# A gated cross-attention and quantized feed-forward block: VectorE's and ScalarE's order in the attention written out, side work cut small, weights rounded on ScalarE

## The chip, the cores and the metric

The kernel runs on one core of one Trainium2 chip. The metric is the device time of one execution in microseconds; lower is better. The engines named below are TensorE (PE, the matmuls; PEld is its weight load), VectorE (DVE), ScalarE (ACT), GpSimd (POOL) and SyncE (SP, which here issues nearly all DMAs). Each engine executes its own list of instructions in order and waits on semaphores for the others.

## The reference

x has 4096 rows (2 x 2048) of 512 numbers, the context 2 x 77 rows of 512. Two gated residual steps follow each other:

```python
x = x + tanh(g_xattn) * attention(layernorm(x), ctx, ctx)      # 16 heads of 32, 77 keys, all fp32
x = x + tanh(g_ffn)   * ffn(layernorm(x))
# ffn: qlinear(512 -> 2048), exact gelu, qlinear(2048 -> 512), where
#   scale = max(max|x|, 1e-6) / 127 ;  xq = round(x / scale)   # one scale for a whole tensor
#   qlinear = (xq @ wq.T + b) * (s_w * s_x)
```

Four one-number scales are needed: of the normalized input of the feed-forward, of its hidden values, and of the weights w1 and w2. Each needs the maximum over its whole tensor before anything of it can be rounded.

## The kernel before, in words

The rows are cut into NB = 8 blocks of 512, each of NT = 4 tiles of 128 rows. The kernel has three stages: the attention of all blocks (within `with actx`), the first feed-forward matmul of all blocks (`ph`, line 664), and the second (`pf`, line 728).

The attention is a pipeline. A loop over blocks i and steps s = 0 to 7 (lines 508 to 577) handles in each step one half (two row tiles) of one group of four heads. In the source, one step does this:

- even s: `apply_v` (378): `pc`, the weights times v for the group before, and ScalarE's copy to `cT`;
- `softmax` (329) for the step two ahead: scores `ps` on PE; on VectorE the maximum `mx` (347) and the difference `e` (351); the exponential on ScalarE (357); on VectorE the sum `sm` (359) and its inverse `rs` (361); the product on GpSimd (362);
- `transpose_a` (368): PE transposes this step's `e` into `pta`, ScalarE copies it to `aT` (376), twice;
- even s: `project_o` (394) of the block before: `po`, and on VectorE the addition to x (404);
- odd s: `project_q` (316) for coming steps: `pq`, and ScalarE's `qT` with its bias (327).

PSUM tiles `pq`, `po`, `pc`, `pk`, `pvv`, `pm` and `pg` share two buffers with the tag `pp`; `pta` and `ptx` share two; `ps` has two.

Beside this pipeline lies side work. `norm(i+2)` (267) takes the mean and variance of a block that comes up (in step 6; that of block 1 in block 0's step 1), and `spread_rstd` sends the inverse deviation through DRAM to a row that `scale_x` (GpSimd) multiplies into the transposed x. `center_wq` (288) takes the column mean off wq once, in block 1. `norm2_stats` and `norm2_max` (408, 413) take mean, variance and the largest normalized value of a finished block, all four tiles at once, in step 7. `weight_step` (454) loads the raw weights piece by piece (1 MB, 128 x 2048 on chip), takes the maximum of each piece (440), gets the scale (`diagonal_of` 174, `scale_of` 182 with the matmul `pg_w`), and rounds by adding and subtracting a magic number: `quantize` (210) does both passes on VectorE (212 in place, 213 to bf16). The raw weights and the blocks of x share eight buffers of one pool; pieces of w2 are loaded, dropped and loaded again.

What sets the order: within `manual_schedule`, the engines named follow the source exactly. In the lead-in (block 0's statistics, transposes and keys) these are VectorE, PE and ScalarE; from line 503 on it is PE alone. There VectorE's, ScalarE's, GpSimd's and SP's instructions are put in order by the framework's scheduler, and `tc.issue_after(ins)` only keeps a piece of side work behind a given instruction of the same engine. The scheduled order is fixed when the program is built.

After the loop, the last block's `po`, statistics and maxima come tile by tile, then the scale `s_x`, the rounding and transposing of block 0 (`xq0`, `px`, `xqT0`), and the feed-forward begins.

Of the kernel before, what the change touches and what calls it, by code (L numbers as in the profile page):

```python
# [15 lines left out]
P = 128  # L16
# [26 lines left out]
def tile_flamingo_gated_block(  # L43
# [115 lines left out]
    xmax = const.tile([P, NB - 1 + NT], F32, name="xmax")  # L159
    hmax = const.tile([P, NB * GT * 2 + 1], F32, name="hmax")  # L160

    def layernorm_stats(xb, mv, rstd, name):

        n = xb.shape[1]
        st = small.tile([P, n, 6], F32, tag="st", name=f"st_{name}")
        for t in range(n):
            nc.vector.bn_stats(st[:, t, :], xb[:, t, :])  # L167
            nc.vector.bn_aggr(mv[:, t, :], st[:, t, :])
        ve = small.tile([P, n], F32, tag="ve", name=f"ve_{name}")
        last = nc.vector.tensor_scalar(ve, mv[:, :, 1], EPS, None, ALU.add).ins  # L170
        nc.gpsimd.tensor_tensor(rstd, ve, mhalf[:, :n], ALU.pow)  # L171
        return last

    def diagonal_of(maxima, name):

        m = const.tile([P, 1], F32, name=f"m_{name}")
        nc.vector.tensor_reduce(m, maxima, AX.X, ALU.max)  # L177
        diag = small.tile([P, P], F32, tag="diag", name=f"diag_{name}", bufs=1)
        nc.vector.tensor_scalar(diag, ident, m, None, ALU.mult)
        return diag  # L180
# [38 lines left out]
    with actx:  # L219
# [44 lines left out]
        rstd_row = {}  # L264
        ln, xnT, qT, aT, cT, es = {}, {}, {}, {}, {}, {}

        def norm(i):

            mv = small.tile([P, NT, 2], F32, tag="mv", name=f"mv{i}")
            rstd = small.tile([P, NT], F32, tag="rstd", name=f"rstd{i}")  # L270
            layernorm_stats(X[i], mv, rstd, f"a{i}")
            ln[i] = mv, rstd
# [15 lines left out]
        def center_wq():  # L288

            total = work.tile([P, D], F32, tag="xn", name="wq_total")  # L290
            nc.gpsimd.tensor_tensor(total, wq_sb[:, 0, :], wq_sb[:, 1, :], ALU.add)
            for kc in range(2, KC):
                nc.gpsimd.tensor_tensor(total, total, wq_sb[:, kc, :], ALU.add)
            pm = ps_p.tile([P, D], F32, tag="pp", name="pm")
            nc.tensor.matmul(pm, ones, total, start=True, stop=True)
            for kc in range(KC):
                w = wq_sb[:, kc, :]
                nc.vector.scalar_tensor_tensor(w, pm, -1.0 / D, w, ALU.mult, ALU.add)

        def transpose_x(i, t):  # L300
            mv, rstd = ln[i]
            if t == 0:
                xnT[i] = work.tile([P, KC, TB], F32, tag="xnT", name=f"xnT{i}", bufs=2)
            xn = work.tile([P, D], F32, tag="xn", name=f"xn{i}_{t}")
            nc.vector.tensor_scalar(
                xn, X[i][:, t, :], mv[:, t, 0:1], rstd[:, t : t + 1], ALU.subtract, ALU.mult
            )
            pt = ps_t.tile([P, KC, P], F32, tag="pt", name=f"ptx{i}_{t}")
            for kc in range(KC):
                nc.tensor.transpose(pt[:, kc, :], xn[:, kc * P : (kc + 1) * P], ident)  # L310
# [18 lines left out]
        def softmax(i, s):  # L329
# [19 lines left out]
            e4 = e.rearrange("p u (j k) -> p u j k", j=HG)  # L349
            last = {}  # L350
            last["DVE"] = nc.vector.tensor_tensor(  # L351
# [4 lines left out]
            ).ins  # L356
            last["ACT"] = nc.scalar.activation(e, e, AF.Exp, scale=SCALE).ins  # L357
# [4 lines left out]
            last["POOL"] = nc.gpsimd.tensor_tensor(  # L362
                e4, e4, rs[:, :, :, None].to_broadcast([P, 2, HG, NK]), ALU.mult
            ).ins
            es[i, s] = e4
            return last
# [27 lines left out]
        def project_o(i, t):  # L394
            po = ps_p.tile([P, D], F32, tag="pp", name=f"po{i}_{t}")
            for g in range(NG):
                nc.tensor.matmul(  # L397
                    po,
# [5 lines left out]
            nc.vector.scalar_tensor_tensor(  # L404
                X[i][:, t, :], po, tg[:, 0:1], X[i][:, t, :], ALU.mult, ALU.add
            )

        def norm2_stats(i, t0=0, t1=NT):
            return layernorm_stats(
                X[i][:, t0:t1, :], mean2[:, i, t0:t1, :], rstd2[:, i, t0:t1], f"f{i}_{t0}"  # L410
            )

        def norm2_max(i, t0=0, t1=NT):

            tm = small.tile([P, NT], F32, tag="tm", name=f"tm{i}_{t0}")
            for t in range(t0, t1):
                xn = work.tile([P, D], F32, tag="xn", name=f"xf{i}_{t}")
                normalize2(xn, i, t)
                nc.vector.tensor_reduce(  # L419
                    tm[:, t - t0 : t - t0 + 1], xn, AX.X, ALU.max, apply_absolute_value=True  # L420
                )
            k = i if t1 - t0 == NT else NB - 1 + t0
            return nc.vector.tensor_reduce(
                xmax[:, k : k + 1], tm[:, : t1 - t0], AX.X, ALU.max
            ).ins
# [4 lines left out]
        wraw, wmax, wdiag = {}, {}, {}  # L430

        def load_w(name, src, pieces):
            for j in pieces:
                wraw[name, j] = big(f"raw_{name}{j}")
                nc.sync.dma_start(wraw[name, j], kchunks(src(j)))

        def weight_max(name, j):
            if j == 0:
                wmax[name] = const.tile([P, 4], F32, name=f"max_{name}")
            nc.vector.tensor_reduce(  # L440
                wmax[name][:, j : j + 1],
                wraw[name, j],
                AX.XY,
                ALU.max,
                apply_absolute_value=True,
            )

        def w1_piece(j):
            return w1T[:, j * TB : (j + 1) * TB]

        def w2_piece(j):
            return w2T[j * TB : (j + 1) * TB, :]

        def weight_step(i, s):
            j, odd = divmod(s, 2)
            if i == 1 and odd:
                weight_max("w1", j)
            if i in (2, 4) and s == 0:
                name = "w1" if i == 2 else "w2"
                s_w[name], inv_w[name] = scale_of(wdiag[name], name, ps_p, "pp")  # L460
            if i == 2 and odd:
                quantize(w1q[:, :, j * TB : (j + 1) * TB], wraw["w1", j], inv_w["w1"])
            if i == 3 and odd:
                weight_max("w2", j)
                if j < 2:
                    load_w("w2", w2_piece, [j + 2])
                else:
                    load_w("w2", w2_piece, [j - 2])
            if i in (1, 3) and s == 2 * NG - 1:
                name = "w1" if i == 1 else "w2"  # L470
                wdiag[name] = diagonal_of(wmax[name], name)
            if i == 4 and odd:
                quantize(w2q[:, j * KC : (j + 1) * KC, :], wraw["w2", j], inv_w["w2"])
                if j in (1, 2):
                    load_w("w2", w2_piece, [j + 1])

        ordered = {mybir.EngineType.DVE, mybir.EngineType.PE, mybir.EngineType.Activation}
        with tc.manual_schedule(engines=ordered):
            ln[0] = (
                small.tile([P, NT, 2], F32, tag="mv", name="mv0"),  # L480
                small.tile([P, NT], F32, tag="rstd", name="rstd0"),
            )
            pk = {}
            for t in range(NT + 1):
                if t < NT:
                    layernorm_stats(
                        X[0][:, t : t + 1, :],
                        ln[0][0][:, t : t + 1, :],
                        ln[0][1][:, t : t + 1],
                        f"a0_{t}",  # L490
                    )
                if t > 0:
                    transpose_x(0, t - 1)
                if t in (2, 3):
                    pk[t - 2] = project_k(0, t - 2)
            place_k(0, 0, pk[0])
            pk[2] = project_k(0, 2)
            place_k(0, 1, pk[1])
            project_q(0, 0)
            place_k(0, 2, pk[2])  # L500
            pk[3] = project_k(0, 3)
            place_k(0, 3, pk[3])
        actx.enter_context(tc.manual_schedule(engines={mybir.EngineType.PE}))
        softmax(0, 0)
        softmax(0, 1)
        project_q(0, 1)
        project_v(0)
        for i in range(NB):
            for s in range(2 * NG):
                g, odd = divmod(s, 2)  # L510
                if not odd and s > 0:
                    apply_v(i, g - 1)
                elif not odd and i > 0:
                    apply_v(i - 1, NG - 1)
                if s + 2 < 2 * NG:
                    last = softmax(i, s + 2)
                elif i + 1 < NB:
                    last = softmax(i + 1, s + 2 - 2 * NG)
                for u in range(2):
                    transpose_a(i, s, u)  # L520
                if i == 0 and s == 2:


                    with tc.issue_after(last["ACT"]):
                        nc.scalar.activation(tg, tg, AF.Tanh)
                    with tc.issue_after(last["POOL"]):
# [285 lines left out]
```

## Time and profile before

| | |
|---|---|
| median of 3 runs | 661.34 us (660.38 to 662.39) |
| the profiled execution | 661.28 us |
| its span, first to last instruction | 659.5 us |
| mean granted PE clock | 0.981 |
| attention, to the last `pc` | 0 to 399.7 us |
| first `ph` matmul | 424.9 us |
| first `pf` matmul | 542.6 us |

In the profile, "busy" is the time in which an engine has an instruction under way. A line such as `aT<-pta` reads "writes aT from pta", x8 counts merged instructions, and a bracket at the end of a line gives the idle time of that engine just before, and the instruction on another engine that ended it. Times on a timeline are from the span's start.

### The profile page before, as it was taken

What the parts mean: (1) busy time and instruction counts of PE and PEld (TensorE: products, weight loads), DVE (VectorE), ACT (ScalarE), POOL (GpSimd) and SP (SyncE); (2) the same over time, 40 slices, a digit from 0 to 9 for tenths busy, and PEclk for the clock granted to TensorE, in tenths of its full rate; (3) what the DMA queues carried; (4) which work ended last, traced back from release to release, by engine and by line L of the source; (5) the groups of instructions that cost most, each with busy time, mean ns of one, the idle gap of its engine ahead of it and who ended that gap; (6) DMA issues with size and microseconds to landing.
All of it is one profiled execution on the core that took longest, in us unless ns stands there. A gap on an engine that the chain in (4) does not pass through costs nothing.

```text
span 659.5 us, 8041 instructions
## 1 busy us (share of the span) xinstructions
PE 620.7 (94%) x2954; PEld 311.1 (47%) x2954; DVE 508.3 (77%) x805; ACT 325.8 (49%) x439; POOL 235.7 (36%) x188
## 2 busy tenths in 40 slices
PE   5999999799999799999999999599999979999997
PEld 5556455455445455455455544244444434444443
DVE  5687678968979968957866767899999779877541
ACT  2355444243344243344434341289998879655430
POOL 2147345255264255264363332000000008997000
PEclk9999999899999899999999999699999999999999
DMA  9922220133252233320000000079999208799952
GB/s 282 375 89 72 74 65 0 17 123 132 80 181 76 80 128 129 80 65 1 16 1 1 0 17 0 8 264 326 295 328 348 58 0 341 255 355 347 336 199 80
DMA packets 51454, 92.76 MB, mean 141 GB/s; under 512 B 22155, under 2 KB 26251, under 8 KB 45784
## 3 DMA queue, kind: packets, MB, share of 16 engines
q1 hardware_dynamic: 50312, 91.58, 40.8%
q10 hardware_dynamic: 1104, 0.69, 0.4%
q8 instruction: 23, 0.38, 0.2%
q14 instruction: 15, 0.12, 0.1%
HBM read 57.11 MB, written 31.47 MB: 134 GB/s over the span
## 4 chain that ended last, share of the span: by engine, by line
PE 73%; DVE 22%; POOL 2%; ACT 1%; issue 1%; DMA 1%; DVEq 0%; POOLq 0%; ACTq 0%
PE pf L728 17%; PE ph L664 17%; PE po L397 11%; PE pq L319 11%; PE pta L375 6%; PE ps L338 5%; PE pc L384 3%; DVE e L351 3%; DVE mx L347 3%; DVE st_a L167 2%; DVE tm L419 2%; DVE xf L197 2%; DVE sm L359 2%; DVE st_f L167 2%; PE pk L231 1%; POOL rstd L171 1%
## 5 line engine op out<-in xcount | busy, mean ns | idle before, releaser
L362 POOL TENSOR_TENSOR e<-e,rs 128x616 f32<-128x616 f32 x64 | 78.0, 1220 | 206.3 <-DVE rs L361 169.7
L376 ACT COPY aT<-pta 77x512 f32<-77x512 f32 x128 | 68.5, 582 | 122.0 <-PE pta L375 121.9
L728 PE MATMUL pf<-w2q,hq 128*128 128x512 bf16 x512 | 112.4, 383 | 2.6 <-DVE hq L213 2.0
L397 PE MATMUL po<-wo_sb,cT 128*128 128x512 f32 x256 | 114.8, 593 | 0.0
L664 PE MATMUL ph<-xqT,w1q 128*128 128x512 bf16 x512 | 113.0, 385 | 0.7 <-DVE xqT L604 0.7
L671 ACT ACTIVATE G<-ph,b1s,s 128x512 f32<-128x512 f32 x128 | 99.5, 778 | 15.0 <-PE ph L664 4.3
L319 PE MATMUL pq<-xT,wq_sb 128*128 128x512 f32 x192 | 87.1, 596 | 0.0
L681 DVE TENSOR_REDUCE hmax<-G 128x1 f32<-128x1024 f32 (+1 forms) x65 | 76.8, 1198 | 8.2 <-ACT G L671 8.2
L728 PEld LDWEIGHTS <-hq 128*128 128x128 bf16 x512 | 50.4, 99 | 64.3 <-issue 2.4
L664 PEld LDWEIGHTS <-w1q 128*128 128x128 bf16 x512 | 50.6, 99 | 62.8 <-issue 3.0
L375 PE MATMUL pta<-ident,e 128*77 128x128 f32 x512 | 72.0, 285 | 3.4 <-POOL e L362 3.4
L347 DVE TENSOR_REDUCE mx<-ps 128x8 f32<-128x616 f32 x64 | 50.6, 791 | 28.7 <-PE ps L338 28.4
L397 PEld LDWEIGHTS po<-wo_sb,cT 128*128 128x128 f32 x256 | 46.4, 190 | 48.2 <-issue 46.6
L359 DVE TENSOR_REDUCE sm<-e 128x8 f32<-128x616 f32 x64 | 50.4, 787 | 23.0 <-ACT e L357 22.8
L357 ACT ACTIVATE e<-e 128x616 f32<-128x616 f32 x64 | 45.9, 717 | 41.6 <-DVE e L351 34.4
L375 PEld LDWEIGHTS pta<-ident,e 128*77 128x77 f32 x512 | 57.1, 150 | 15.2 <-issue 9.2
L721 ACT ACTIVATE Gb<-Gb,inv_h 128x2048 f32<-128x2048 f32 x22 | 43.7, 2001 | 35.9 <-DMA Gb<-h 35.9
L338 PEld LDWEIGHTS ps<-kb,qT 64*128 64x128 f32 x512 | 36.5, 188 | 47.9 <-ACT qT L327 24.2
L742 POOL TENSOR_TENSOR x<-x,b_sb 128x512 f32<-128x512 f32 x32 | 57.1, 1824 | 0.1
L351 DVE TENSOR_TENSOR e<-ps,mx 128x616 f32<-128x616 f32 x64 | 51.0, 797 | 3.7 <-DVE m_w L177 0.3
L338 PE MATMUL ps<-kb,qT 64*128 64x154 f32 x512 | 51.4, 321 | 1.4 <-ACT qT L327 1.4
L319 PEld LDWEIGHTS pq<-xT,wq_sb 128*128 128x128 f32 x192 | 35.1, 193 | 34.9 <-issue 34.6
(97 smaller groups left out, 617.6 us busy)
## 6 DMA issues: line engine op xcount, KB each, us to landing
h<-G SPq DMA_DIRECT2D x22, 1024.0 KB, 5.5
Gb<-h SPq DMA_DIRECT2D x22, 1024.0 KB, 8.0
raw_w<-in_w2T SPq DMA_DIRECT2D x8, 1024.0 KB, 6.0
out_y<-x SPq DMA_DIRECT2D x32, 256.0 KB, 3.6
x<-in_x SPq DMA_DIRECT2D x7, 1024.0 KB, 7.0
xT<-in_xT SPq DMA_DIRECT2D x6, 1024.0 KB, 5.6
raw_w<-in_w1T SPq DMA_DIRECT2D x4, 1024.0 KB, 12.8
rrow<-row SPq DMA_DIRECT2D x6, 256.0 KB, 4.9
```

The source lines that it names most:

```text
L319: nc.tensor.matmul(pq, wq_sb[:, kc, g * P : (g + 1) * P], (xnT if i < 2 else xT_sb)[i][:, kc, :], start=(kc == 0), stop=(kc == KC - 1),)
L338: nc.tensor.matmul(ps[:, q, u * RK : (u + 1) * RK], qT[i, g][r, t * P : (t + 1) * P], kblk[i // NBB][r, g, :], start=True, stop=True,)
L347: nc.vector.tensor_reduce(mx, sc, AX.X, ALU.max)
L351: last["DVE"] = nc.vector.tensor_tensor(e.rearrange("p u (q r k) -> p q u r k", q=NR, r=RT), sc, mx[:, :, :, :, None].to_broadcast([P, NR, ...
L362: last["POOL"] = nc.gpsimd.tensor_tensor(e4, e4, rs[:, :, :, None].to_broadcast([P, 2, HG, NK]), ALU.mult).ins
L375: nc.tensor.transpose(pt[:NK, j, :], es[i, s][:, u, j, :], ident)
L376: nc.scalar.copy(aT[i, g][:, :, t * P : (t + 1) * P], pt[:NK, :, :])
L397: nc.tensor.matmul(po, cT[i, g][:, t * P : (t + 1) * P], wo_sb[:, g, :], start=(g == 0), stop=(g == NG - 1),)
L664: nc.tensor.matmul(ph, w1q[:, kc, fc * P : (fc + 1) * P], cur[:, kc, :], start=(kc == 0), stop=(kc == KC - 1),)
L671: nc.scalar.activation(G[:, 2 * v + u, :], ph, AF.Gelu, bias=b1s[:, fc : fc + 1], scale=s1,)
L681: nc.vector.tensor_reduce(hmax[:, k + u : k + u + 1], G[:, 2 * v + u : 2 * v + u + n, :], AX.XY, ALU.max, apply_absolute_value=True,)
L728: nc.tensor.matmul(po[t], hq[:, fc, t * P : (t + 1) * P], w2q[:, fc, :], start=(fc == 0), stop=(fc == FC - 1),)
```

## The change

- VectorE and ScalarE join PE in `manual_schedule` for the whole attention. GpSimd and SP stay with the scheduler.
- `softmax` is split into `scores` (`ps`, `mx`, `e`), `exponential` (ScalarE) and `shares` (`sm`, `rs`, GpSimd's product). Side work stands between them or at the end of the step.
- The addition of `po` (`add_o`) moves from behind its matmuls to the head of the next, odd step on VectorE. Statistics go tile by tile: two tiles of block i+2 in each of steps 4 and 6 (block 1's in steps 0 and 1), one tile of block i-1 in each odd step. Maxima of block i-2 go two tiles at a time in steps 0 and 2. Each tile has its own column of `xmax`, so the reduction that merged four columns falls away. The normalizing of block 1 leaves `transpose_x` and comes in steps 2 and 3.
- Weight work is a table of tasks by the number of the step, k = 8i + s, done at the end of it. The maximum of a piece is taken in two halves.
- The first pass of the rounding moves to ScalarE (`weight_round`); VectorE keeps the second (`weight_integers`).
- `center_wq`: the sum comes in step 0 of block 1; ScalarE copies the mean out of PSUM and GpSimd subtracts it, where VectorE did both in one instruction.
- Loads: x2 and all of w1 stand ahead of the loop in the source, x(i+2) in step 1, and w2 takes six loads where it took eight.

The core of the diff:

```diff
+        def exponential(i, s):
+            e = es[i, s]
+            return nc.scalar.activation(e, e, AF.Exp, scale=SCALE).ins
...
-            for kc in range(KC):
-                w = wq_sb[:, kc, :]
-                nc.vector.scalar_tensor_tensor(w, pm, -1.0 / D, w, ALU.mult, ALU.add)
+            mean = work.tile([P, D], F32, tag="xn", name="wq_mean")
+            nc.scalar.activation(mean, pm, AF.Copy, scale=1.0 / D)
+            for kc in range(KC):
+                w = wq_sb[:, kc, :]
+                nc.gpsimd.tensor_tensor(w, w, mean, ALU.subtract)
...
+        def weight_round(name, j):
+            w = wraw[name, j]
+            nc.scalar.activation(w, w, AF.Copy, bias=MAGIC, scale=inv_w[name])
+
+        def weight_integers(name, j):
...
+            nc.vector.tensor_scalar(dst, wraw[name, j], MAGIC, None, ALU.subtract)
...
+        for j in range(4):
+            for half in range(2):
+                at(4 + 2 * j + half, weight_max, "w1", j, half)
+                at(22 + 2 * j + half, weight_max, "w2", j, half)
+            at(14 + 2 * j, weight_round, "w1", j)
+            at(15 + 2 * j, weight_integers, "w1", j)
+        for name, step in ("w1", 12), ("w2", 30):
+            at(step, weight_diagonal, name)
+            at(step + 1, weight_scale, name)
+        for j, step in enumerate((17, 19, 21, 26)):
+            at(step, load_w, "w2", j)
+        for j, step in (2, 32), (3, 33), (0, 37), (1, 40):
+            at(step, weight_round, "w2", j)
+            at(step + 1, weight_integers, "w2", j)
+        at(34, load_w, "w2", 0)
+        at(38, load_w, "w2", 1)
...
+                if not odd and k > 0:
+                    apply_v(*((i, g - 1) if s > 0 else (i - 1, NG - 1)))
+                if odd and i > 0:
+                    add_o(i - 1, g)
+                if ahead[0] < NB:
+                    scores(*ahead)
                 for u in range(2):
                     transpose_a(i, s, u)
+                if ahead[0] < NB:
+                    last = exponential(*ahead)
...
+                if i > 1 and s in (0, 2):
+                    norm2_max(i - 2, s)
+                    norm2_max(i - 2, s + 1)
...
+                if i + 2 < NB and s in (4, 6):
+                    norm_stats(i + 2, s - 4)
+                    norm_stats(i + 2, s - 3)
+                if ahead[0] < NB:
+                    last = shares(*ahead)
                 if not odd and i > 0:
                     project_o(i - 1, g)
                 if s in (1, 3):
                     project_q(i, g + 2)
...
+                for task, args in tasks.get(k, ()):
+                    task(*args)
+                if s == 1 and i > 0 and i + 2 < NB:
+                    load_x(i + 2)
...
+                if i == 1 and s == 0:
+                    total = sum_wq()
+                if i == 1 and s == 3:
+                    center_wq(total)
```

In the last block the maxima of block 6 come in steps 4 and 6 and its fourth tile after the loop. After the loop, VectorE's and ScalarE's order is again that of the source: per tile `po`, `add_o`, statistics, and the maximum of the tile before.

## The prediction, on record before the result was known

> **What bounds the kernel now.** I read the page first, for the balance of the engines.
>
> ```profile
> PE 620.7 (94%) x2954; PEld 311.1 (47%) x2954; DVE 508.3 (77%) x805; ACT 325.8 (49%) x439; POOL 235.7 (36%) x188
> ```
>
> TensorE (PE) is busy for 94% of a span of 659.5 us. The profiled execution took 661.28 us, 1.8 us more than its span, and the median of three is 661.34, so a microsecond of span is a microsecond of result. The change edits only the attention, so I need what PE loses there. I number the steps k = 8i + s. The next view is the busy time per stretch, cut where PE starts the first `pc` of blocks 1 to 7 (columns: stretch, length, then busy us and count of PE, PEld, DVE, ACT, POOL; clock, DMA share, GB/s).
>
> ```profile
> 69.14:115.48 46.34, 46.34 (x227) 23.68 (x226) 35.90 (x55) 19.35 (x32) 21.78 (x18) 1.00 0.11 29
> 115.48:166.65 51.17, 47.58 (x227) 24.95 (x227) 42.60 (x76) 19.35 (x32) 21.56 (x18) 0.97 0.27 88
> 166.65:214.27 47.62, 45.63 (x226) 23.33 (x225) 40.94 (x69) 19.13 (x32) 22.48 (x18) 1.00 0.33 117
> 214.27:265.44 51.17, 47.57 (x227) 24.79 (x226) 42.81 (x76) 19.35 (x32) 21.57 (x18) 0.97 0.33 108
> 265.44:313.07 47.63, 45.64 (x226) 23.34 (x225) 34.91 (x66) 19.09 (x32) 22.42 (x18) 1.00 0.19 51
> 313.07:359.78 46.71, 45.55 (x225) 23.30 (x224) 31.86 (x61) 19.11 (x32) 21.52 (x18) 1.00 0.03 6
> ```
>
> Where PE never waits, a pair of steps takes 11.37 us (`pc` to `pc` in the PE timeline, 132.53 to 143.91), so a block takes 4 x 11.37 = 45.48. Block 1 is that plus its `pm` matmul. Blocks 2 to 6 lose 5.7, 2.1, 5.7, 2.1 and 1.2 us; block 7 loses 0.3 before its last pairs. That is 17.2 us, and more cannot be won in the loop. The PE timeline shows the shape of a large loss:
>
> ```profile
> 118.14 3.60 PE L397 MATMUL po<-wo_sb,cT 128*128 128x512 f32 x8
> 125.33 0.46 PE L186 MATMUL pg_w<-diag_w,ones 128*128 128x128 f32 x2 [3.59 <-DVE xmax L423]
> 125.72 1.30 PE L338 MATMUL ps<-kb,qT 64*128 64x154 f32 x8
> 126.94 1.99 PE L375 MATMUL pta<-ident,e 128*77 128x128 f32 x8
> 128.73 3.88 PE L319 MATMUL pq<-xT,wq_sb 128*128 128x512 f32 x8
> ```
>
> PE stood for 3.6 us before the one-column scale of w1 and then ran 8 `pta` in 1.99 us instead of 1.10: the stall also slows what follows. What VectorE (DVE) did meanwhile:
>
> ```profile
> 119.96 0.80 DVE L351 TENSOR_TENSOR e<-ps,mx 128x616 f32<-128x616 f32 x1 [0.33 <-DVE m_w L177]
> 120.70 1.00 DVE L197 TENSOR_SCALAR xf<-x,mean,rstd 128x512 f32<-128x512 f32 x2
> 121.61 1.27 DVE L419 TENSOR_REDUCE tm<-xf 128x1 f32<-128x512 f32 x2
> 122.80 0.99 DVE L197 TENSOR_SCALAR xf<-x,mean,rstd 128x512 f32<-128x512 f32 x2
> 123.71 1.27 DVE L419 TENSOR_REDUCE tm<-xf 128x1 f32<-128x512 f32 x2
> 124.90 0.28 DVE L179 TENSOR_SCALAR diag_w<-ident,m_w 128x128 f32<-128x128 f32 x1
> 125.16 0.78 DVE L359 TENSOR_REDUCE sm<-e 128x8 f32<-128x616 f32 x1
> ```
>
> A whole block's maxima stand ahead of `diag_w` and of a softmax sum `sm`. DVE is at 42.6 of 51.2 us here: busy without a pause from about 106 to 132, idle elsewhere. So it is the piling up at the border that costs. The 2.1 us losses (`pta` waits 1.73 for POOL's `e`, late for the same reason at 180.6) and the 1.2 (`ps` waits for ACT's `qT`) are of that kind.
>
> **The change part by part.**
>
> *Side work spread (DVE order).* Costs are taken from starts of neighbours in the DVE timeline: softmax `mx`, `e`, `sm`, `rs` 2.55 a step; `add_o` 0.78; one tile's bn_stats and aggr 0.82 (0.2 more with `ve`); one tile's `xf` and its maximum 1.20; `sm` waits 0.78 for the exponential when nothing lies between. Half a weight maximum is bounded by half of L440's 2.27 and by the 1.20 of L681's row, which has just that shape: I take 1.12 net of overlap. A weight cast (L213) is 1.21, 1.13 net. An even step with two tiles of maxima costs 2.55 + 2.40 = 4.95; an odd one 2.55 + 0.78 + 0.78 + 0.82 = 4.93, and 6.06 with a cast. Summed by the new list, blocks 1 to 7 want 42, 44, 47, 42, 40, 37, 33 us of DVE against PE's 45.5. Only steps 22 to 27 exceed a pair's 11.37: 11.8, 12.1, 12.3. DVE is then about 2 us behind PE and catches up in steps 28 to 31 (11.4, 10.8). What cushions it: `ps(k+2)` is made in step k and `pta(k+2)` comes one pair later, while the chain ps, mx, e, exp, sm, rs, POOL is 6 to 7.5 us, which leaves 4 to 5. The tighter cushion is ACT's order: in an odd step `qT` stands behind the exponential, which ends about 2.7 us after `ps`, while `pq` ends 4.5 after it; 2 us of lag is just covered. I charge 0.3 us (0 to 3).
> The six merging L423 reduces vanish (0.9 us of DVE, hidden).
>
> *What the stalls become.* All 17.2 go, but PE must still do two `pg_w` (0.46 each): 16.3 gained. `pg_w` now follows `pq` in steps 13 and 31 with `diag_w` a step earlier. With two `pp` buffers the next `pc` then waits for `qT` (0.69 after `pq`): 0.5 us twice, 1.0 (0 to 2). DVE's wait for `pg_w` blocks only the next `mx`, whose `ps` is later on PE.
>
> *ScalarE rounds the weights.* Eight instructions of 128x2048 f32: ACT's row L721 has that form at 2.00 us, so ACT gains 16 us; DVE loses eight of L212 at 1.74, 13.9 us. The Trainium skill speaks against it: "ScalarE: Activation LUTs", rules for kernel authors, sends multiply and add to VectorE, and prices ScalarE at about 0.3 us plus 0.83 ns per element, an estimate of 2.0 us which L721 confirms. By that rule each move costs 0.3 us. By the block rows it costs nothing as a sum (ACT 19 of 45.5 us) and without it DVE would want 49 us in block 2, where three of the rounds fall; the place on the queue decides. Rounds at the end of even steps (14, 16, 18, 20, 32, 40) run under the 3.5 us of `po`, before `aT` is wanted. Those in odd steps 33 and 37 stand between `qT` and the next `cT`: `cT` ends about 3.5 us after `pq` (`qT` 0.8, round 2.0, `cT` 0.6) and `po` wants it at 2.7 (`pc` 1.0, `ps` 0.73, `pta` 0.93), so PE waits 0.9 us twice: 1.8 (0 to 4). The nearest row for such short waits, the 1.73 us before `pta`, shows no slower matmuls after it.
>
> *Centring wq.* DVE loses four L298 (2.5 us). ACT makes a copy (0.6), POOL four subtractions at 1.27 (L293's row). In step 11 POOL has `e` (ends 93.8 on the old clock), two `scale_x` and these four: 7.6 us, to 101.4; PE wants wq for `pq` of block 2 at 100.6. I charge 0.9 us, once (0, to 3.3 if the next `e` and an `add_bias` go first).
>
> *Block 0.* `norm_stats` of block 1 comes in steps 0 and 1, ahead of the sums. x1 was issued at 11.6 and took at most 9.3 us, so it is there by 31. Walking DVE's durations from 29.1: sum 3 ends at 38.3 instead of 35.8, POOL does the power (1.0) then `e`, ready at 40.0, and `pta` was at 39.4: 0.6 us lost (0 to 2).
>
> *Loads.* SP issued x2 and three w1 pieces at 17.5 to 23 already and the fourth at 60.6, when wk_sb came free; the new place in the source is the same queue behind the same release. Two of eight w2 loads vanish. The reloads at 34 and 38 follow the casts that free their buffers; 6 us to landing against 10 us or more to their rounds. x6 at 33 has 11 us until step 36. `spread_rstd` stays in step 6, its row and broadcast used four steps on. I charge 0; if one were late it would hold all of ACT or DVE, by its lateness (0 to 2).
>
> *Tail.* Two merging reduces fall off the last chain and the feed-forward's DVE work no longer sits among the `xqT` copies: 0.3 gained (0 to 0.8). Its chain otherwise stands: last `po`, statistics, maximum, `pg_x`.
>
> Sum: 16.3 + 0.3 - 0.3 - 1.0 - 1.8 - 0.9 - 0.6 = 12.0 us. 661.3 - 12.0 = 649.3.
>
> **The rivals.**
> *The stalls go and nothing replaces them.* All charges zero: 16.3 + 0.8 = 17: 644.3. For it: cushions of 4 us. Against: `cT` and the `pp` order are arithmetic. Chance 0.14.
> *New in-order waits eat half.* Charges near their upper ends in two or three places (centring 3, rounds 4, lag 3): gain near 5, 656. For it: each charge is a queue whose order can be worse than I read it. Against: they would have to go wrong together. Chance 0.13.
> *Slower: DVE becomes the bound in blocks 2 to 5.* Their sums are 44, 47, 42 and 40 us, 172.5 together, against PE's 182. If each of the 32 steps costs DVE w more than the sum (waits for `po` before `add_o`, for the exponential behind a queue on ACT), PE loses 172.5 + 32w - 182 - 4, the 4 being the cushion, spent once. That eats the 12.0 us from w = 0.8; at 1.0 it is 18.5 and gives 668. For it: DVE was busy all of 106 to 132, and three engines are now strict queues. Against: in that stretch its instructions followed each other without gaps, so w is small when there is work. Chance 0.08.
> *The order hardly differs from what the scheduler chose.* 661. The moved maxima alone contradict it. Chance 0.03.
>
> **How the numbers follow.** Likeliest 649.3, chance 0.62 (646 to 653). The range takes in the free case's edge and the half case's: 644 to 656.5. Under 0.3% (2 us) is about what a measurement of this kernel can't tell from no change. Faster: 0.62 + 0.14 + 0.13 = 0.89; same 0.03; slower 0.08.
>
> **What would show it.** Blocks 2 to 6 should each take 45.5 to 48 us between first `pc`s; no PE gap over 2 us from 70 to 390; no slow `pta`; no wait for L423. Short gaps should stand before `po` in steps 34 and 38 (ACT `cT`) and before the first `pq` of block 2 (POOL `wq_sb`). DVE should be near 491 us busy, ACT near 342. It is wrong if PE waits in most steps of blocks 2 to 4 for `e` or `qT`, or if a weight load holds ACT.

## The result, and the profile after

The changed kernel takes 652.15 us (median of 6 runs, 651.03 to 653.89) against 661.87 before (6 runs): a ratio of 0.9856, 95% interval 0.9831 to 0.9881, so 1.4% less time. 649.3 had been forecast, in a range of 646 to 653. The profiled execution took 651.43 us with a span of 649.6, against 661.28 and 659.5.

The page's first part, for the changed kernel:

```profile
PE 616.6 (95%) x2933; PEld 309.3 (48%) x2954; DVE 511.1 (79%) x798; ACT 340.9 (52%) x448; POOL 244.3 (38%) x200
```

ScalarE has its 15 us more. VectorE, which gave up eight passes, is busier than before, not the 17 us less that the forecast named. The busy time per stretch, cut as before at the first `pc` of blocks 1 to 7:

```profile
68.75:115.87 47.12, 46.64 (x229) 24.09 (x229) 37.19 (x67) 21.82 (x34) 27.95 (x24) 1.00 0.20 43
115.87:161.36 45.49, 45.49 (x225) 23.30 (x224) 40.39 (x66) 25.01 (x35) 23.22 (x19) 1.00 0.40 122
161.36:210.25 48.89, 46.14 (x228) 23.63 (x228) 43.99 (x78) 19.57 (x33) 23.42 (x21) 1.00 0.23 71
210.25:255.74 45.49, 45.49 (x225) 23.30 (x225) 37.20 (x65) 23.69 (x34) 22.00 (x18) 1.00 0.26 79
255.74:305.85 50.11, 47.16 (x226) 24.68 (x225) 37.34 (x68) 21.11 (x33) 22.58 (x20) 0.97 0.26 66
305.85:351.34 45.49, 45.49 (x226) 23.30 (x225) 31.84 (x55) 19.34 (x32) 20.88 (x19) 1.00 0.04 6
```

The granted clock (third number from the end) is 1.00 except in block 5. Blocks 2, 4 and 6 run at PE's own pace. Blocks 3 and 5 lose 3.4 and 4.6 us, block 1 0.8. The waits of PE in the loop, longest total first (engine, line, for whom, us, times, longest):

```profile
PE pc L409 <- ACT aT L401: 4.3, 3, 2.8
PE pc L409 <- DVE g_w L189: 2.7, 2, 2.2
PE ps L357 <- ACT qT L345: 0.4, 1, 0.4
PE pq L337 <- POOL xT L294: 0.2, 1, 0.2
```

No old wait is left except 1.4 us of `pc` for `aT` in the last block, which both kernels have. The rest is new. Where the 9.9 us of span come from, by pairs of steps measured from `pc` to `pc`: 17.2 us of old stalls gone; 8.8 us of new ones (steps 12: 0.8, 28: 0.9, 30: 2.5, 40: 2.9, 42: 1.7; those of 12 and 30 have PE's own `pg_w` in them); 0.4 won ahead of block 1, 0.55 won between the last `pc` and the first `ph`. The remaining 0.6 lie in the feed-forward, whose instructions the edit leaves alone; why is not followed here.

Two new stalls can be read off directly. First the one of pairs 40 and 42: the DMA issues of SP, and ScalarE's rounding of the w2 piece in step 40:

```profile
251.81 0.37 SPq L285 DMA_DIRECT2D row<-rstd  x1
252.28 0.45 SPq L459 DMA_DIRECT2D raw_w<-in_w2T  x1
```

```profile
259.31 0.72 ACT L378 ACTIVATE e<-e 128x616 f32<-128x616 f32 x1
267.00 2.00 ACT L481 ACTIVATE raw_w<-raw_w,inv_w 128x2048 f32<-128x2048 f32 x1 [6.97 <-DMA raw_w<-in_w2T]
268.91 1.04 ACT L401 COPY aT<-pta 77x512 f32<-77x512 f32 x2
```

The load landed 14.6 us after its issue. ScalarE stood 7 us for it with `aT` behind, and PE with it:

```profile
263.58 3.60 PE L337 MATMUL pq<-xT,wq_sb 128*128 128x512 f32 x8
270.00 1.06 PE L409 MATMUL pc<-aT,vb 77*32 77x512 f32 x8 [2.82 <-ACT aT L401]
271.20 1.40 PE L357 MATMUL ps<-kb,qT 64*128 64x154 f32 x8
272.52 1.99 PE L400 MATMUL pta<-ident,e 128*77 128x128 f32 x8
```

Again `pta` is slow after the stall, 1.99 us, at a granted clock of 0.72 (270 to 276 us). The other stall is that of pair 30, where `pc` waits for VectorE's `g_w`:

```profile
207.67 0.38 PE L187 MATMUL pg_w<-diag_w,ones 128*128 128x128 f32 x2
210.25 1.07 PE L409 MATMUL pc<-aT,vb 77*32 77x512 f32 x8 [2.19 <-DVE g_w L189]
```

VectorE comes to the scale late in step 31, because it has the statistics of a tile to do first:

```profile
207.47 0.80 DVE L385 TENSOR_REDUCE sm<-e 128x8 f32<-128x616 f32 x1 [0.78 <-ACT e L378]
208.30 0.20 DVE L387 RECIPROCAL rs<-sm 128x8 f32<-128x8 f32 x1
208.42 0.64 DVE L165 BATCH_NORM_STATS2 st_f<-x 128x6 f32<-128x512 f32 x1
209.09 0.18 DVE L166 BATCH_NORM_AGGREGATE mean<-st_f 128x2 f32<-128x6 f32 x1
209.31 0.60 DVE L172 TENSOR_SCALAR ve_f<-mean 128x2 f32<-128x2 f32 x1
209.82 0.28 DVE L189 TENSOR_REDUCE g_w<-pg_w 128x1 f32<-128x128 f32 x1
```

`pg_w` was there at 208.05 (207.67 + 0.38). The first of these lines holds a third trouble: 0.78 us of VectorE idle before `sm`.

### The profile page after: what moved, and what is told of

It reads as the page before. It is cut to its first block, busy times and chain, and to the rows that moved or that the text cites. A ratio compares the mean times of both kernels' runs of the same rounds, so it can differ in the third digit from the quotient of the medians.

```text
span 649.6 us, 8028 instructions
## 1 busy us (share of the span) xinstructions
PE 616.6 (95%) x2933; PEld 309.3 (48%) x2954; DVE 511.1 (79%) x798; ACT 340.9 (52%) x448; POOL 244.3 (38%) x200
## 4 chain that ended last, share of the span: by engine, by line
PE 80%; DVE 13%; DMA 3%; ACT 2%; issue 1%; POOL 0%; DVEq 0%; ACTq 0%
PE pf L780 17%; PE ph L716 17%; PE po L422 14%; PE pq L337 12%; PE pta L400 7%; PE ps L357 6%; PE pc L409 4%; DMA raw_w<-in_w2T 2%; DVE e L368 2%; DVE mx L366 2%; DVE max_w L465 2%; DVE st_a L165 1%; DVE sm L385 1%; PE pk L232 1%; PE pvv L256 1%
## 5 line engine op out<-in xcount | busy, mean ns | idle before, releaser
L389 POOL TENSOR_TENSOR e<-e,rs 128x616 f32<-128x616 f32 x64 | 79.3, 1240 | 169.5 <-DVE rs L387 75.8
L716 PE MATMUL ph<-xqT,w1q 128*128 128x512 bf16 x501 | 111.0, 381 | 1.4 <-DVE xqT L656 0.7
L400 PEld LDWEIGHTS pta<-ident,e 128*77 128x77 f32 x512 | 56.4, 149 | 11.8 <-issue 9.5
## 6 DMA issues: line engine op xcount, KB each, us to landing
raw_w<-in_w1T SPq DMA_DIRECT2D x4, 1024.0 KB, 12.3
```

The lines of the kernel that those rows point to most:

```text
L389: return nc.gpsimd.tensor_tensor(e4, e4, rs[:, :, :, None].to_broadcast([P, 2, HG, NK]), ALU.mult).ins
L400: nc.tensor.transpose(pt[:NK, j, :], es[i, s][:, u, j, :], ident)
L716: nc.tensor.matmul(ph, w1q[:, kc, fc * P : (fc + 1) * P], cur[:, kc, :], start=(kc == 0), stop=(kc == KC - 1),)
```

## The experiments

Times are medians, ratios are to the kernel before, timed alongside, with 95% intervals. "Pair 30" is steps 30 and 31, from `pc` to `pc`; what it loses is its time over 11.37 us in the profiled execution.

**Three stalls, taken away one by one.** My theory: each new stall has a local cause in the new order.

*e1* puts the reload ahead of the row store of block 6:

```diff
+                if i == 4 and s == 6:
+                    with tc.issue_after(wload[0]):   # the load of this step
+                        spread_rstd(i + 2)
```

> Only the order of two DMAs on SP changes, in step 38: the reload of the w2 piece goes ahead of the 2 KB store of block 6's inverse deviations. Theory Q (the 1 MB load took 14.6 us to land because it stood in the queue behind that store of single numbers, whose own landing takes 9 us): the load lands in 5 to 7 us, ScalarE's 7.0 us wait in step 40 goes, and so do the 2.9 and 1.7 us that PE loses in the pairs 40 and 42: about 4.6 us faster than the changed kernel, near 647.5. Theory M (the memory or the DMA engines are slow at that moment, or the two steps left are too short): it lands in 12 us or more again and nothing is won. Either way block 6's scaling in step 42 must not come late.

647.59 us, 0.9799 (0.9781 to 0.9816). The profiled execution:

```profile
251.42 0.37 SPq L459 DMA_DIRECT2D raw_w<-in_w2T  x1
251.88 0.46 SPq L285 DMA_DIRECT2D row<-rstd  x1
```

```profile
258.93 0.72 ACT L378 ACTIVATE e<-e 128x616 f32<-128x616 f32 x1
259.55 1.99 ACT L483 ACTIVATE raw_w<-raw_w,inv_w 128x2048 f32<-128x2048 f32 x1
```

The load lands in 5.3 us, ScalarE doesn't wait, and pairs 40 and 42 take 11.37 and 11.38. Theory Q holds: 4.6 us hung on the order of two DMAs issued half a microsecond apart.

*e2* moves the scale ahead of the statistics in steps 13 and 31:

```diff
+                if k in (13, 31):
+                    weight_scale("w1" if k == 13 else "w2")
                 if odd and i > 0:
                     norm2_stats(...)
```

> In steps 13 and 31 the scale (the matmul pg_w and VectorE's reading of it) stands ahead of the tile statistics instead of behind them. Theory V (pc waits 2.19 us for the PSUM buffer that VectorE frees late, because it is behind PE and has statistics to do first): the wait in step 31 falls by the 1.4 us of statistics, in step 13 its 0.5 goes: 1.5 to 2 us faster than the changed kernel, near 650.3. Rival S (the wait is the chain pg_w, semaphore, reduction, which the order cannot shorten): under 0.5 us.

650.49 us, 0.9851 (0.9828 to 0.9874). The medians can't tell this from the changed kernel (0.9856), so the evidence is the pair: pair 30 loses 1.05 instead of 2.50, as theory V says, and `pc` waits less for the same `g_w`:

```profile
208.44 1.07 PE L409 MATMUL pc<-aT,vb 77*32 77x512 f32 x8 [0.75 <-DVE g_w L189]
```

Pair 12 keeps its 0.77, so there the short wait is the chain itself (S).

*e3* spreads the maxima one tile to a step:

```diff
-                if i > 1 and s in (0, 2):
-                    norm2_max(i - 2, s)
-                    norm2_max(i - 2, s + 1)
+                if i > 1 and s < NT:
+                    norm2_max(i - 2, s)
```

> Maxima of a finished block come one tile in each of steps 0 to 3 instead of two tiles in steps 0 and 2. The same VectorE work, but in odd steps it now fills the 0.78 us in which VectorE waited for the exponential. Theory L (the stalls in pairs 28 and 30 come from VectorE's lag, which builds up in steps 22 to 27 where a pair costs 11.8, 12.1 and 12.3 us): the pairs fall to 11.8, 11.3, 11.5, the lag at step 28 from 2 us to 0.6, pair 28 loses its 0.9 us and pair 30 about 1.5 of its 2.5: 2 to 2.5 us faster than the changed kernel, near 649.8. Rival S (the stalls are dependencies that do not hang on the lag): no change.

649.48 us, 0.9831 (0.9801 to 0.9861). This interval, too, overlaps that of the changed kernel; by the pairs, pair 28 loses nothing now: that was VectorE's lag (L). Pair 30 still loses 1.97, not the 1.0 I expected; the lag has less part in it than the order that e2 changes.

*e4* has the three together.

> The three edits together. If each is its own cause they add, the second and third in part for the same wait: 4.6 + 2.9 us, near 644.5, with every pair of steps from 14 to 60 at 11.4 us. If a further limit stands behind them (VectorE's sums, POOL), less than 5 us in all.

644.31 us, 0.9751 (0.9733 to 0.9768). They add, and no further limit shows. All pairs from 14 to 58 take 11.4 us but pair 30, which has `pg_w`.

**Which part of the change brings the gain?** Theory O/W asked whether order or relief of VectorE does it.

*e5*: VectorE does the first pass again, at the same places.

```diff
-            nc.scalar.activation(w, w, AF.Copy, bias=MAGIC, scale=inv_w[name])
+            nc.vector.tensor_scalar(w, w, inv_w[name], MAGIC, ALU.mult, ALU.add)
```

> The changed kernel with the first rounding pass back on VectorE, at the same places in the table: its order and small pieces kept, 8 x 1.7 us given back to VectorE, 16 us taken off ScalarE. Theory O (the gain is the order and the small pieces): most of the 10 us stays; block 2 then wants 49 us of VectorE against 45.5, so 3 to 6 us come back there and in block 3, and the wait for the late w2 piece moves to VectorE: 654 to 657. Theory W (the gain is the 14 us of work taken from VectorE): it goes back to about 661.

660.75 us, 0.9982 (0.9970 to 0.9994). Nearly all of the gain is gone, as W says; O had said 654 to 657. PE's longest waits in the loop:

```profile
PE ps L357 <- ACT qT L345: 4.5, 4, 1.8
PE pc L409 <- DVE x L432: 3.0, 1, 3.0
PE pc L409 <- DVE g_w L189: 2.7, 2, 2.2
PE pq L337 <- POOL xT L294: 1.2, 2, 1.0
```

These are mostly followers of a late VectorE: `qT` behind a late exponential, a late `add_o` that still holds a PSUM buffer. The profiled execution took 662.7 us, more than the median; in its pair 32 PE also ran at a lower clock (see the last section).

*e6*: the kernel before, with only ScalarE's rounds.

```diff
+        def quantize_w(dst, src, inv):   # for w1 and w2
+            nc.scalar.activation(src, src, AF.Copy, bias=MAGIC, scale=inv)
+            nc.vector.tensor_scalar(dst, src, MAGIC, None, ALU.subtract)
```

> The kernel before with one thing of the change: ScalarE does the first rounding pass. Theory W: near 652. Theory O: the two losses of 5.7 us stand ahead of any rounding and stay; the 2.1 us at the ends of blocks 2 and 4, where a rounding piece adds to the pile, may go: 657 to 662.

666.72 us, 1.0063 (1.0044 to 1.0083): slower, and outside both theories, so W fails here. The two large stalls stayed (pairs 16 and 32: 5.7 each), pairs 36, 40 and 42 lose 1.4, 3.2 and 1.0, and ScalarE stands 2.2 us for a w2 piece ahead of an exponential.

*e7*: the changed kernel, but VectorE's and ScalarE's order left to the scheduler behind the lead-in; each piece on VectorE is tied behind its step's `e`.

```diff
-            tc.manual_schedule(engines={PE, DVE, Activation})
+            tc.manual_schedule(engines={PE})
+                with tc.issue_after(diff[0]):   # diff[0]: the step's e; around the maxima, statistics and tasks
```

> The changed kernel with its small pieces and ScalarE's rounding, but VectorE's and ScalarE's order left to the scheduler behind the lead-in, each piece tied behind its step's difference e as side work was before. If the pieces do it, about 652 again. If the written order does it, 656 to 661: the scheduler can again put several pieces ahead of a softmax sum.

648.20 us, 0.9769 (0.9745 to 0.9793). The pieces do it without the written order (still with ScalarE's rounds). Its runs spread from 646.4 to 654.9. The profile is of the slowest: pair 40 loses 8.5 us there, since the scheduler had put the rounding ahead of `qT`, and the load took 9.3 us.

*e8*: the kernel before with its pieces, VectorE's and ScalarE's order taken from its source (line 503: the three engines in place of PE alone).

> The kernel before, pieces as they were, with VectorE's and ScalarE's order taken from its source. If the order alone does it, faster than 661. If the pieces are needed, slower: step 7 then holds 3.5 + 8.7 us of statistics and maxima in front of the next mx in six blocks, and two-pass rounding of 3.4 us in steps; PE's cushion is 4 to 5 us, so some 6 us lost per block, near 680.

727.89 us, 1.0991 (1.0967 to 1.1016). From VectorE's timeline at the end of block 1, first and last lines of a pile:

```profile
130.04 0.20 DVE L361 RECIPROCAL rs<-sm 128x8 f32<-128x8 f32 x1
130.16 0.64 DVE L167 BATCH_NORM_STATS2 st_f<-x 128x6 f32<-128x512 f32 x1
...
142.13 0.29 DVE L179 TENSOR_SCALAR diag_w<-ident,m_w 128x128 f32<-128x128 f32 x1
142.33 0.79 DVE L347 TENSOR_REDUCE mx<-ps 128x8 f32<-128x616 f32 x1
```

Twelve microseconds without softmax work; 7 to 10 us of PE lost at most block ends. With the large pieces, the source's order is harmful.

*e9* is e7 with the reload ahead of the store, as in e1, and ScalarE's rounds tied behind their step's exponential.

> As the run with the pieces in the scheduler's order, with two ties more: the w2 reload ahead of block 6's row store on SP, and each piece on ScalarE (the rounds) behind its step's exponential. Theory P (small pieces placed by the step, and rounds on ScalarE, make the gain; the written order adds little): the 8.5 us stall of pair 40, where the rounding had been put ahead of qT and waited 6.2 us for its data, goes: 645 to 648. If the written order is worth something of its own, it stays at 650 or above.

644.80 us, 0.9744 (0.9726 to 0.9763). The stall of pair 40 is gone, as theory P says.

*e10* is e4 with VectorE's rounds.

> The best version so far (644.3) with the first rounding pass back on VectorE. Theory B (it is VectorE's sum per pair against PE's 11.37 us that decides): one tile of maxima a step has freed 1.6 us per block, a round costs 1.15 to 1.7 net, so block 2 wants 46 to 48 us against 45.5 and block 4 about 44 to 46: 645 to 648. Rival R (VectorE's rounds cost for another reason, such as their place ahead of add_o or POOL being held up by them): the 9 us between the changed kernel and its version with VectorE's rounds are lost here too: near 653.

647.16 us, 0.9781 (0.9759 to 0.9803): the move is worth 2 to 3 us here, not 8 to 9. That is B's range, but R is not ruled out in its part on GpSimd: the longest wait of PE left is one of 1.6 us for GpSimd's `xT` in pair 20, and there GpSimd's product `e` took 2.06 us beside VectorE's rounding pass, where it takes 1.22 in e4 (see the last section).

*e11* is e7 with VectorE's rounds: the small pieces, without the other two parts.

> The small pieces alone: VectorE does both rounding passes, VectorE's and ScalarE's order is the scheduler's, pieces tied behind their step's difference e. With the runs before, this completes the table of order, pieces and ScalarE's rounds. If pieces alone make the gain: 648 to 653. If they need ScalarE's rounds, as in the written order: 657 to 661.

644.98 us, 0.9758 (0.9729 to 0.9787). This is the turn of the study: the pieces alone give more than the whole change, and ScalarE's rounds, without which the written order had nearly nothing left, are not needed. Most of the 7 us between the two, though, is the DMA of e1: the scheduler happened to issue the reload ahead of the store,

```profile
248.61 0.37 SPq L459 DMA_DIRECT2D raw_w<-in_w2T  x1
249.78 0.37 SPq L285 DMA_DIRECT2D row<-rstd  x1
```

so pairs 40 and 42 lose nothing here and 4.6 us in the changed kernel. Pairs 28 and 30 lose 0.8 instead of 3.4, pair 12 loses 1.5 instead of 0.8. What VectorE's order has to do with it, in e5 above all, its waits in the loop show: in the changed kernel, in e11, and in the kernel before.

```profile
DVE sm L385 <- ACT e L378: 30.1, 32, 5.8
DVE mx L366 <- PE ps L357: 19.1, 16, 1.9
```

```profile
DVE mx L366 <- PE ps L357: 44.0, 24, 2.7
...
DVE sm L385 <- ACT e L378: 1.6, 2, 0.8
```

```profile
DVE sm L359 <- ACT e L357: 20.6, 26, 0.8
```

The written order leaves VectorE idle for the exponential 32 times. e11's order puts something between `e` and `sm` in nearly every step, and its waits are the harmless kind, for scores that PE hasn't made yet. It is not the scheduler as such that does this: in the kernel before it left 26 such waits. Small pieces tied behind each `e` give it something to put there. Nor does the wait cost anything where VectorE has time to spare: e4 keeps 20 of them (15.7 us) and is as fast as e11. From e11:

```profile
170.52 0.80 DVE L368 TENSOR_TENSOR e<-ps,mx 128x616 f32<-128x616 f32 x1
171.24 0.68 DVE L165 BATCH_NORM_STATS2 st_f<-x 128x6 f32<-128x512 f32 x1
171.84 1.20 DVE L465 TENSOR_REDUCE max_w<-raw_w 128x1 f32<-128x1024 f32 x1
172.95 0.78 DVE L385 TENSOR_REDUCE sm<-e 128x8 f32<-128x616 f32 x1
```

*e12* tests that in the written order: e5 with the statistics of odd steps moved ahead of the sum, and e1's swap.

```diff
+                if odd and i > 0:
+                    norm2_stats(i - 1, g, ...)
                 if ahead[0] < NB:
                     last = shares(*ahead)
...
-                if odd and i > 0:
-                    norm2_stats(i - 1, g, ...)
```

> The changed kernel with VectorE's rounds (660.75 so far), with two edits: in odd steps the tile statistics of the finished block stand between the difference e and the sum sm, where VectorE waited 0.78 us for the exponential, instead of behind the sum; and the w2 reload goes ahead of the row store, so that its late landing takes no part. Theory F (the written order made VectorE idle in every odd step, 30 us in all in the changed kernel, and only that made ScalarE's rounds necessary): the stalls of pairs 20 to 32, 10.4 us together, nearly go as well as the 7.6 us of pairs 40 and 42: 645 to 648. If only the reload mattered: about 653.

645.23 us, 0.9750 (0.9726 to 0.9774). VectorE's wait for the exponential falls from 25.1 us to 3.9, and of the 10.4 us that pairs 20 to 32 lost in e5 only pair 30's 0.8 stay (1.2 come in pair 36). The 7.6 us of pairs 40 and 42 go with the swap. Theory F holds.

| order of VectorE, ScalarE | pieces | first rounding pass | us |
|---|---|---|---|
| scheduler | large | VectorE (before) | 661.9 |
| scheduler | large | ScalarE (e6) | 666.7 |
| source | large | VectorE (e8) | 727.9 |
| scheduler | small | VectorE (e11) | 645.0 |
| scheduler | small | ScalarE (e7; e9 with two ties) | 648.2; 644.8 |
| source | small | VectorE (e5; e12 with the wait filled and the swap) | 660.8; 645.2 |
| source | small | ScalarE (the change; e4 with three edits) | 652.2; 644.3 |

"Small" takes in the new places of the loads and of the maxima of the normalized values, and the centring of wq; these were not tried apart. In the scheduler's order the small pieces are always tied behind their step's `e`; no run has them untied. e4, e9, e11 and e12 can't be told from each other by these intervals.

## Why the prediction was right, and where its steps failed

*What bounds the kernel.* Right. All 17.2 us of old stalls went.

*The charges.* 4.6 us were forecast and about 7.5 came (the 8.8 of new stalls, less PE's own two `pg_w`, which the forecast had taken off the gain, less the 0.4 won in block 0). Hardly one term was right by itself; the total is near because errors of both signs met, and that is luck.

- ScalarE's rounds in steps 33 and 37: charged 1.8, measured 0. The step that failed is "`cT` ends about 3.5 us after `pq` (...) and `po` wants it at 2.7". `cT` did end late, after the start of `po` at 247.02 (step 38):

```profile
245.06 1.99 ACT L481 ACTIVATE raw_w<-raw_w,inv_w 128x2048 f32<-128x2048 f32 x1
246.95 0.57 ACT L417 COPY cT<-pc 128x512 f32<-128x512 f32 x1
```

  But `po` didn't want it: `project_o(i - 1, g)` reads the `cT` of the block before, and the one made in step 38 belongs to block 4, whose `po` comes a block later. Only in step 0 does the newest `cT` matter, and there for the last quarter of `po`. I took neighbours in the source for a dependency.
- The loads: charged 0, measured 4.6 (pairs 40 and 42). The step that failed is "6 us to landing against 10 us or more": the median of the w2 row was used without asking what stands ahead in the queue, though the paragraph itself names `spread_rstd` in the same step. e1 shows it.
- VectorE's lag: charged 0.3, measured 0.9 in pair 28, in the place forecast (steps 22 to 28; e3). The bound of 3 held. The sum of VectorE was right to a few tenths: the pairs 22, 24 and 26 took 12.1, 11.9 and 12.6 us from `mx` to `mx`, against 11.8, 12.1 and 12.3. Its 0.78 us of waiting in odd steps stood in that sum as a cost; I didn't see that it could be filled.
- `pg_w`: its own 0.9 and 1.0 of waiting were charged, 1.9 together; the two pairs lose 3.3. The step that failed is "the next `pc` then waits for `qT`": it waits for VectorE's `g_w` (e2), which in step 31 stands behind a tile's statistics on a VectorE that is late already.
- Centring: charged 0.9, measured 0. GpSimd ended its four subtractions at 100.1, not at 101.4, because its `e` ended at 92.1 and not at 93.8; `pq` began at 100.2, so there is hardly a margin.
- Block 0: charged 0.6. The wait that was forecast is there, `pta` for GpSimd's `e` at 39.07, but it takes 0.26 us; the first `pc` comes 0.7 us earlier than before, and 0.4 of it is left at block 1. What won the 0.7 was not followed.
- The tail: 0.3 forecast, 0.55 measured.

*Its own signs.* Of those named beforehand, ScalarE's busy time (341 us) came, and the waits for L423 are gone; the others did not come. Blocks 3 and 5 took 48.9 and 50.1 us, not 45.5 to 48; PE had gaps of 2.19 and 2.82 us where none over 2 was to be; `pta` was slow once; the short gaps before `po` and before the first `pq` of block 2 are absent. And of the two signs of being wrong one came: "a weight load holds ACT", for 6.97 us.

*VectorE's busy time.* 491 us were forecast, 511 came. By the rows of the two profiles the work given away did go, 18 us of it. But rows that stayed grew by 14.7 us together: `ve_f` from 2.2 to 8.7 (most of them now 0.60 us each), the casts of the weights from 9.6 to 11.9, `mv` and `mean` from 9.2 to 11.6, the tiles' maxima from 20.6 to 22.0, and smaller ones. The rest is that neighbours overlap 6 us less. Why the rows grew stays open.

*The rivals.* The slower case, VectorE as the bound, did not come. But e5 shows how near it was: with the rounds back on VectorE, the gain is gone. The waits of 0.78 us in odd steps were in the sums already; in this order ScalarE's rounds were what kept VectorE from being the bound. The case "the order hardly differs" was put badly: the question was not whether it differs but whether it is better, and it is worse.

## What to carry to other kernels

Cut side work to pieces that fit the slack of one step and tie each to its step; with the few edits that went with it, that was worth 16 us here (e11), and neither the engine move (e9) nor the order written by hand (e4, e12) added anything that these intervals show. If you do write an engine's order and the engine is short of time, put side work into the waits of the chain (here between the difference and the sum), or the idle time that you write in becomes load. Before a load is called hidden, look at what is issued just ahead of it on its queue, and before a wait is charged, check by its index which tile the consumer reads.

## What the runs showed of the hardware

The 2 KB store of single numbers (`row`, that of block 6) took 10.0 to 12.2 us to land. A 1 MB load issued 0.5 us behind it landed after 14.2 to 15.6 us in four runs; issued 0.5 to 1.2 us ahead of it, after 5.1 to 6.2 us in six and 9.3 in one (e7), which I can't explain.

VectorE's 128x2048 rounding pass took 1.23 to 1.78 us in e5 and 1.61 to 2.00 in the kernel before, the same instruction on other neighbours. GpSimd's work beside it can be the one that takes longer: in e5 five of the eight passes had one of GpSimd's products begin 0.25 us after their start, and these products took 2.05 to 2.06 us, against a median of 1.22. In the kernel before and in e11 no product took more than 1.38.

PE can run slower after a stall, but the length of the wait alone does not decide it. After 2.82 us in the changed kernel `pta` took 1.99 us; after 2.60 us in e2 it took 1.10, at a granted clock of 1.00. After the 2.19 us of pair 30 the changed kernel kept its clock of 1.00 and a `pta` of 1.10; in e5, after the same wait at the same place, the clock was 0.50 for 6 us:

```profile
214.46 1.94 PE L409 MATMUL pc<-aT,vb 77*32 77x512 f32 x8 [2.19 <-DVE g_w L189]
217.65 1.99 PE L400 MATMUL pta<-ident,e 128*77 128x128 f32 x8
```

What else decides is not shown here. It is part of what a late load costs: in the profiles of e2 and e3 the reload was as late as in the changed kernel (14.4 and 14.2 us) and pair 40 lost 2.7 and 2.5, but pair 42 lost 0.2 where the changed kernel lost 1.7.
